# One RNN, one state-space layer, one LSTM and one adapter in a software pipeline: the RNN's lead goes from 56 to 54 steps and the side jobs move to other steps

## The chip, the core and the metric

The kernel runs on one core of one Trainium2 chip. The metric is the device time of one launch in microseconds (us), as the median of several runs. A profile of one execution stands beside it. In it PE is TensorE's matmuls, PEld its weight loads, DVE is VectorE, ACT is ScalarE, POOL is GpSimd and SP the engine that issues most of the DMAs. A line such as L402 is line 402 of the kernel.

## What is computed

The input `x` has 4 sequences of 1024 tokens with 512 features. Four layers follow each other, each added to its input: a tanh RNN, a state-space layer, an LSTM, and an adapter whose weights depend on the condition vector. Cut to what matters, for `h`, `state` and `c` carried from token to token:

```python
# 1. RNN
h = tanh(x_t @ Wx + b + h @ Wh)
# 2. state space; the convolution has the condition vector's rows as its 4 taps
proj = conv(x) @ Wp + bp;  B_t = softplus(proj[:N]);  C_t = tanh(proj[N:])
u = x @ Ws + bs
state = decay * state + dt * B_t * u_t;  y_t = C_t * state;  out = y @ Wo + bo
# 3. LSTM
A = x_t @ Wx + b + h @ Wh
i, f, o, g = sigmoid(A[0:H]), sigmoid(A[H:2H]), sigmoid(A[2H:3H]), tanh(A[3H:4H])
c = f * c + i * g;  h = o * tanh(c)
# 4. adapter: one 512x512 matrix per sequence
out = x @ (base + a(cond) @ b(cond))
```

Everything is float32. The RNN and the LSTM are recurrences of 1024 steps over only 4 rows, so the number of steps and the time of one step set the time of the kernel.

## The kernel before

Time is cut into 32 chunks of `TC` = 32 steps. `do_pass(c)` walks the 32 steps of chunk `c` of the LSTM. The RNN runs `LEAD` = 56 steps ahead of it: in step `t` of pass `c` it does its step number `32c + t + 56`. Before the LSTM has anything to do, one short pass (number -2, 24 steps) and one whole pass (number -1, 32 steps) advance the RNN alone; this prologue also loads weights and computes the adapter's matrices. In pass `c` the layers are staggered: the LSTM works on chunk `c`, the state-space layer on chunk `c + 1`, the RNN's input projections (`project0`) on chunk `c + 3`, the adapter on chunk `c - 1`.

The program's order is written by hand: each engine does its instructions in the order in which the code issues them, and waits where an operand is not there. An LSTM step is cut into two halves of the hidden width, A and B (`Half`, L392). One step issues, in this order (L846 to L898):

- TensorE: the LSTM's 96 bfloat16 matmuls (`lstm_mm`, L374), those of A first as far as A's own h reaches, then those that need B's h; then the step's "pe" jobs; then the RNN's 16 float32 matmuls (`rnn_mm`, L348). In the first steps of the prologue `keep_busy` adds matmuls whose result nobody reads.
- VectorE: for each half a transpose of the accumulator (L402), a sum (L408), the products and the cell (L428, L433), the new h (L441), and h split into bfloat16 parts (L207). Half A's and half B's are interleaved. Behind B's cell come the step's "gap" jobs, then B's h and its splits, then the RNN's transpose and addition (`rnn_pre`, L365), then the "end" jobs. The first instruction of the next step is A's transpose.
- ScalarE: the gates (L415), A's tanh (L438), B's gates, then "gap" jobs, then two copies of the next step's input sums (`lstm_input`, L389), then B's tanh, then the RNN's tanh (L371), then "end" jobs.

A job is a triple of step, place ("pe", "gap" or "end") and function. `do(t, place)` runs those that match, in the order of the list: the adapter's, then the state-space layer's, then the LSTM's input projections of the next chunk, then `load_x`, then `project0`, then the LSTM's input projections of the running chunk. The jobs that the change touches are these:

- `ssm_jobs` (L451): `add` forms the state-space input from x and the RNN's h (L460). `taps` and `skip` are its matmuls. On ScalarE follow L498 and L499, then the exponential L500 and the copy L501, and the output's tanh L502. On VectorE follow four reciprocals of 64x32 (`turn`, L494), two products (L503, L504), and a chain of 14 operations: six of a series (L509), L511, L512, L513, four scans (L516), and the output y (L521). Then come 16 matmuls (`out_mm`) and four additions (`x2_end`, L533).
- `input_jobs` (L797): the LSTM's input projections for eight steps of a chunk: four groups of matmuls (L333), two transposes (`input_turn`, L337), two bias additions of two gates each (`input_bias`, L345). The first eight steps of a chunk are prepared in the pass before it, the others in the same pass.
- `project0` (L309): four groups of 16 matmuls, each with a copy on ScalarE (L321).
- `at_step(i, f)` (L680) puts a job of the prologue at the i-th step counted from the start, which needs `LEAD` to find the pass.

The places of the state-space layer's VectorE work come from two lines:

```python
place = lambda n: ("gap", "end", "end")[n % 3]
jobs += [(19 + (n + 1) // 3, place(n + 1), f) for n, f in enumerate(chain)]
```

Of the kernel before, what the change touches and what calls it, by code (L numbers as in the profile page):

```python
# [10 lines left out]
AF = mybir.ActivationFunctionType  # L11
# [5 lines left out]
KC = D // P  # L17
TC = 32
NCHUNK = T // TC
TOK = TC * B  # L20
TG = 8
LEAD = TC + 24
CT = 32
TAPS = B
NG = 4 * KC
# [1 line left out]
NS = 64  # L27
# [8 lines left out]
SERIES = [1.0 / (2 * n + 1) for n in range(1, 8)]  # L36
# [3 lines left out]
def cond_resid_kernel(ctx: ExitStack, tc: tile.TileContext, a: dict, out: bass.AP):  # L40
# [79 lines left out]
    x1 = state.tile([P, KC, 3 + TC, B], F32, name="x1", tag="x1")  # L120
# [18 lines left out]
    vec = const.tile([P, 4], F32, name="vec", tag="vec")  # L139
# [161 lines left out]
    def bank(name, shape, tag="fill", bufs=2):  # L301
        return psum.tile(shape, F32, name=name, tag=tag, bufs=bufs)

    def tiled(dst, columns, x, first=True, final=True, tiles=4):

        for j in range(tiles):
            nc.tensor.matmul(dst[CT * j : CT * (j + 1)], columns(j), x, start=first, stop=final)  # L307
# [143 lines left out]
    def ssm_jobs(c):  # L451
        x, h, po = xin[c % XBUFS], h0[c % 2], {}
        v, act = nc.vector, nc.scalar

        def sm(name):
            return small.tile([NS, TOK], F32, name=name, tag=name, bufs=1)

        def add(ms, t0, t1):
            t = lambda y: y[:, ms, t0:t1].rearrange("p c t b -> p c (t b)")
            v.tensor_add(t(x1[:, :, 3:, :]), t(x), t(h))  # L460


        jobs = [
            (5, "end", lambda: add(slice(0, 2), 0, TC - 4)),
            (6, "end", lambda: add(slice(2, 4), 0, TC - 4)),
            (7, "end", lambda: add(slice(0, 4), TC - 4, TC)),
        ]
        pb = bank("pb", [P, 2, TOK], tag="pb", bufs=1)


        def taps(k):
            for tap in range(TAPS):
                tiled(
                    pb[:, 0, :], lambda j: wp[:, tap, k, CT * j : CT * (j + 1)], x1[:, k, tap : tap + TC, :],
                    tap == 0 and k == 0, tap == TAPS - 1 and k == KC - 1,
                )

        def skip():
            for k in range(KC):
                tiled(  # L480
                    pb[:, 1, :], lambda j: ws[:, k, CT * j : CT * (j + 1)], x1[:, k, 3:, :],
                    k == 0, k == KC - 1, tiles=NS // CT,
                )

        cg, z, e, u, w, p = (sm(n) for n in ("cg", "z", "e", "u", "w", "p"))
        bt, vv, states, y = z, e, w, p
        v3, y3 = (t.rearrange("p (t b) -> p t b", b=B) for t in (vv, states))
        y_last = y3[:, TC - 1, :]
        jobs += [(8 + 2 * k, "pe", lambda k=k: taps(k)) for k in range(KC)]
        jobs.append((16, "pe", skip))  # L490

        def turn(n):
            cols = slice(n * TOK // 4, (n + 1) * TOK // 4)
            v.reciprocal(u[:, cols], u[:, cols])  # L494


        jobs += [
            (14, "end", lambda: act.activation(z, pb[:NS, 0, :], AF.Identity, bias=vec[:NS, 0:1])),  # L498
            (14, "end", lambda: act.activation(e, pb[:NS, 0, :], AF.Abs, bias=vec[:NS, 0:1])),  # L499
            (15, "end", lambda: act.activation(e, e, AF.Exp, scale=-1.0)),  # L500
            (15, "end", lambda: act.activation(u, e, AF.Copy, bias=2.0)),  # L501
            (18, "end", lambda: act.activation(cg, pb[NS:, 0, :], AF.Tanh, bias=vec[NS:, 0:1])),  # L502
            (18, "end", lambda: v.tensor_mul(u, u, e)),  # L503
            (18, "end", lambda: v.tensor_mul(w, u, u)),  # L504
            (18, "end", lambda: act.activation(p, w, AF.Copy, scale=2.0 * SERIES[-1])),
            (24, "end", lambda: act.copy(s1, y_last)),
        ]

        chain = [lambda q=q: v.scalar_tensor_tensor(p, p, 2.0 * q, w, ALU.add, ALU.mult) for q in SERIES[-2::-1]]  # L509
        chain += [  # L510
            lambda: v.scalar_tensor_tensor(p, p, 2.0, u, ALU.add, ALU.mult),  # L511
            lambda: v.scalar_tensor_tensor(bt, z, 0.0, p, ALU.max, ALU.add),  # L512
            lambda: v.scalar_tensor_tensor(vv, pb[:NS, 1, :], vec[:NS, 1:2], bt, ALU.add, ALU.mult),  # L513
        ]
        for b in range(B):
            chain.append(lambda b=b: v.tensor_tensor_scan(  # L516
                y3[:, :, b], decay, v3[:, :, b], s1[:, b : b + 1], ALU.mult, ALU.add
            ))

        chain += [  # L520
            lambda: v.scalar_tensor_tensor(y, states, dt, cg, ALU.mult, ALU.mult),  # L521
        ]
        place = lambda n: ("gap", "end", "end")[n % 3]
        jobs += [((16, "end"), (16, "end"), (17, "gap"), (17, "end"))[n] + (lambda n=n: turn(n),) for n in range(4)]
        jobs += [(19 + (n + 1) // 3, place(n + 1), f) for n, f in enumerate(chain)]

        def out_mm():
            po[0] = bank("ssm_out", [P, KC, TOK], tag="po", bufs=1)
            for m in range(KC):
                tiled(po[0][:, m, :], lambda j: wo[:, P * j + CT * m : P * j + CT * (m + 1)], y)  # L530

        def x2_end(m):
            v.scalar_tensor_tensor(  # L533
                x2[c % 2][:, m].rearrange("p t b -> p (t b)"), po[0][:, m, :], bo[:, 0, m : m + 1],
                x1[:, m, 3:, :].rearrange("p t b -> p (t b)"), ALU.add, ALU.add,
            )

        jobs += [
            (24, "pe", out_mm),
            *((24 + (m + 1) // 2, ("end", "gap")[m % 2], lambda m=m: x2_end(m)) for m in range(KC)),  # L540
            (26, "end", lambda: act.copy(x1[:, :, 0:3, :], x1[:, :, TC : TC + 3, :])),
        ]
        return jobs

# [64 lines left out]
    def adapt_w2(j):  # L609

        half, hd, rg = j // (KC * RANK // WR), j // (RANK // WR) % KC, j % (RANK // WR) // 2
        ps = bank("pp", [P, P])
        for k in range(KC):
            for t in range(4):
                nc.tensor.matmul(  # L615
                    ps[CT * t : CT * (t + 1), :], hid[:, k, :], w2[j + t // WR][:, t % WR, k],
                    start=(k == 0), stop=(k == KC - 1),
                )
        nc.scalar.copy(xr[:, half, hd, rg], ps)
        for n in range(j + W2_BUFS, min(j + W2_BUFS + 2, NW2)):  # L620
            load_w2(n)
# [55 lines left out]
    def at(c, t, f):  # L677
        early.setdefault((c, t), []).append(f)

    def at_step(i, f):  # L680

        c, t = divmod(i - LEAD, TC)
        at(c, t, f)
# [48 lines left out]
    for j in range(0, NW2, 2):  # L732
        f = lambda j=j: adapt_w2(j)
# [63 lines left out]
    def input_jobs(c, n, steps, turns):  # L797
        ps = {}

        def mm(k):  # L800
            if not ps:

                ps[0] = bank("proj2", [P, D], tag=("ada", "po")[n % 2], bufs=1)
            input_mm(c, n, k, ps[0])

        work = (
            lambda: input_turn(c, n, 0, ps[0]), lambda: input_turn(c, n, 2, ps[0]),
            lambda: input_bias(c, n, 0), lambda: input_bias(c, n, 2),
        )
        return [(t, "pe", lambda k=k: mm(k)) for k, t in enumerate(steps)] + [  # L810
            (t, place, f) for (t, place), f in zip(turns, work)
        ]


    def do_pass(c, first=0, src=None, dst=None, last=None):

        lstm = c >= 0
        jobs = []
# [5 lines left out]
        if -1 <= c < NCHUNK - 1:  # L824
            jobs += ssm_jobs(c + 1)
            jobs += input_jobs(
                c + 1, 0, range(25, 29), ((28, "end"), (29, "gap"), (29, "end"), (30, "gap"))
            )
        if src is not None:
            jobs.append((9, "end", lambda: load_x(c + 4, src)))  # L830
        if c + 3 < NCHUNK:
            for m in range(KC):
                mm, end = project0(c + 3, m)
                t = (18, 20, 22, 30)[m]
                jobs += [(t, "pe", mm), (t, "end", end)]
        if lstm:
            jobs += input_jobs(c, 1, range(4), ((3, "end"), (4, "gap"), (4, "end"), (5, "gap")))
# [8 lines left out]
        for t in range(first, TC):  # L846
            r = divmod(c * TC + t + LEAD, TC)
            rnn = r[0] < NCHUNK
# [54 lines left out]
    for m in range(KC):  # L903
        mm, end = project0(0, m)
        mm()
        end()
    def dst(c):
        return lambda b: out[b, bass.ds(c * TC, TC), :]

    do_pass(-2, first=2 * TC - LEAD)  # L910
    for c in range(-1, NCHUNK):
        if c == 0:
            for m in range(2):
                lstm_input(0, 0, m)
        do_pass(
            c, src=a["xT"][c + 4] if c + 4 < NCHUNK else None, dst=dst(c - 1) if c > 0 else None,
            last=dst(c) if c == NCHUNK - 1 else None,
        )
# [60 lines left out]
```

## Time and profile before

| what | value |
|---|---|
| median of 3 runs | 4686.77 us (4686.28 to 4688.5) |
| profiled execution | 4682.72 us, of which the span is 4680.9 us |
| granted TensorE clock, mean | 0.998 |
| LSTM matmuls (L383) | 98304, busy 2900.4 us |
| RNN matmuls (L352) | 32768, busy 1088.6 us |
| LSTM input projections (L333) | 4096, busy 529.6 us |
| transposes of the accumulator (L402) | 4096, mean 309 ns |
| first transpose of the first LSTM step | 157.8 us from the start |
| first transpose of the last LSTM step | 4667.2 us from the start |

The span is the time from the first to the last instruction that the profile shows; the execution adds 1.8 us around it. The last two rows give the main loop: 1023 steps in 4509.4 us. A matmul of float32 is recorded as two. Busy times are unions over an engine, and ends of matmuls are modelled, so an engine that is shown busy all the time need not be at its limit. A bracket at the end of a line of the timeline gives the idle time of that engine ahead of the instruction, and what ended it.

### The profile page before, as it was taken

To read this page: it belongs to the slowest core of one execution; us is meant where nothing else is said; L and a number is where in the kernel's file an instruction comes from. 1 tells how busy PE (TensorE), PEld (TensorE's weight loads), DVE (VectorE), ACT (ScalarE), POOL (GpSimd) and SP (SyncE) were. 2 spreads that over 40 slices of the span, in tenths; PEclk is the share of its full clock that TensorE was granted. 3 is DMA by queue.
4 is the path that set the end of the run, shared out by engine and by line. 5 is a ranking of instruction groups with operands and counts; after the bars stand their busy time and mean duration, and the time that the engine had idled before them with its cause. 6 is when DMAs were issued, how large, how long until landed. Compare 5 with 4: busy or idle time off the path is not lost.

```text
span 4680.9 us, 326427 instructions
## 1 busy us (share of the span) xinstructions
PE 4546.1 (97%) x146816; PEld 3574.0 (76%) x146816; DVE 3951.6 (84%) x22102; ACT 1876.8 (40%) x9693; POOL 47.9 (1%) x92
## 2 busy tenths in 40 slices
PE   7999999999999999999999999999999999999986
PEld 4777777777777777777777777778777777777754
DVE  4688888888888888888888888888888888888876
ACT  3334444444443444443444444444444444444333
POOL 3000000000000000000000000000000000000000
PEclk9999999999999999999999999999999999999999
DMA  6300000000000000000000000000000000000000
GB/s 151 123 6 8 9 7 9 9 7 9 9 7 9 9 7 9 9 7 9 9 7 9 9 7 9 9 7 9 9 7 9 9 7 9 9 5 7 6 6 8
DMA packets 40235, 67.77 MB, mean 14 GB/s; under 512 B 8864, under 2 KB 26016, under 8 KB 38320
## 3 DMA queue, kind: packets, MB, share of 16 engines
q1 hardware_dynamic: 35792, 46.55, 3.7%
q8 instruction: 1147, 18.79, 1.7%
q14 instruction: 256, 2.10, 0.2%
q0 software_dynamic: 1696, 0.19, 0.0%
q10 hardware_dynamic: 1344, 0.14, 0.0%
HBM read 38.34 MB, written 8.39 MB: 10 GB/s over the span
## 4 chain that ended last, share of the span: by engine, by line
PE 91%; DVE 7%; issue 1%; POOL 0%; DMA 0%; ACT 0%; SPq 0%; DVEq 0%; ACTq 0%; POOLq 0%
PE acc L383 55%; PE acc L352 18%; PE proj L333 9%; PE pb L307 3%; DVE tt L402 3%; DVE gc L408 2%; PE proj L307 2%; PE ada L754 2%; DVE prod L428 1%; PE ssm_out L307 1%; DVE h L207 1%; PE idle L307 0%; PE pp L615 0%; DVE h L441 0%; DVE tt L367 0%
## 5 line engine op out<-in xcount | busy, mean ns | idle before, releaser
L383 PE MATMUL acc<-wh,h 128*12 128x256 bf16 x98304 | 2900.4, 273 | 95.0 <-DVE h L207 92.0
L383 PEld LDWEIGHTS <-h 128*12 128x12 bf16 x98304 | 2312.5, 87 | 545.5 <-DVE h L207 181.9
L402 DVE STREAM_TRANSPOSE tt<-acc 128x192 f32<-128x192 f32 (+1 forms) x4096 | 1233.0, 309 | 285.9 <-PE acc L383 261.5
L415 ACT ACTIVATE gc<-gc 128x24 f32<-128x24 f32 (+1 forms) x4096 | 855.3, 216 | 1386.1 <-DVE gc L408 1379.4
L352 PEld LDWEIGHTS acc<-wh,h 128*4 128x4 f32 x32768 | 808.3, 87 | 507.3 <-issue 204.6
L352 PE MATMUL acc<-wh,h 128*4 128x128 f32 x32768 | 1088.6, 273 | 17.3 <-ACT h L371 12.8
L408 DVE TENSOR_REDUCE gc<-tt 128x24 f32<-128x96 f32 (+1 forms) x4096 | 1037.4, 255 | 70.5
L207 DVE TENSOR_TENSOR h<-h 128x8 f32<-128x8 f32 (+1 forms) x4098 | 671.6, 164 | 69.9
L371 ACT ACTIVATE h<-pre 128x16 f32<-128x16 f32 x1024 | 221.5, 216 | 1126.1 <-DVE pre L368 1126.1
L438 ACT ACTIVATE th<-gc 128x8 f32<-128x8 f32 x2048 | 427.7, 209 | 255.1 <-DVE gc L433 220.1
L333 PE MATMUL proj<-wx,x 128*32 128x512 f32 x4096 | 529.6, 592 | 0.0
L441 DVE SCALAR_TENSOR_TENSOR h<-gc,th 128x8 f32<-128x8 f32 x2048 | 328.5, 160 | 143.6 <-ACT th L438 134.0
L367 DVE STREAM_TRANSPOSE tt<-acc 128x128 f32<-128x128 f32 x1024 | 315.4, 308 | 64.7 <-PE acc L352 64.6
L428 DVE SCALAR_TENSOR_TENSOR prod<-gc 128x16 f32<-128x16 f32 x2048 | 347.7, 170 | 12.6
L390 ACT COPY tt<-xw 128x32 f32<-128x32 f32 x2048 | 327.7, 207 | 0.0
L433 DVE SCALAR_TENSOR_TENSOR gc<-prod 128x8 f32<-128x8 f32 x2048 | 297.4, 145 | 0.0
L368 DVE TENSOR_TENSOR pre<-xw,tt 128x16 f32<-128x16 f32 x1024 | 179.6, 175 | 37.6
L307 PE MATMUL proj<-xin,wx 128*32 128x128 f32 x4096 | 135.1, 274 | 12.0 <-DMA wh<-in_Wh_dram 11.9
L307 PE MATMUL pb<-x,wp 128*32 128x128 f32 x4096 | 136.1, 274 | 1.1 <-issue 0.7
L754 PE MATMUL ada<-layer,x 128*32 128x512 f32 (+1 forms) x1056 | 133.9, 586 | 2.7 <-DVE x L747 2.6
L307 PEld LDWEIGHTS proj<-xin,wx 128*32 128x32 f32 x4096 | 114.7, 111 | 15.9 <-DMA wh<-in_Wh_dram 11.9
L333 PEld LDWEIGHTS proj<-wx,x 128*32 128x32 f32 x4096 | 118.8, 110 | 5.5 <-issue 0.3
(125 smaller groups left out, 1161.6 us busy)
## 6 DMA issues: line engine op xcount, KB each, us to landing
layer<-in_w2T_dram SPq DMA_DIRECT2D x32, 512.0 KB, 4.7
xin<-in_xT_dram SPq DMA_DIRECT2D x128, 64.0 KB, 2.5
out_dram<-x SPq DMA_DIRECT2D x124, 64.0 KB, 2.1
wx<-in_Wx_dram SPq DMA_DIRECT2D x20, 256.0 KB, 5.1
layer<-in_Wh_dram SPq DMA_DIRECT2D x16, 256.0 KB, 4.9
wh<-in_Wh_dram SPq DMA_DIRECT2D x4, 256.0 KB, 8.1
layer<-in_w_dram SPq DMA_DIRECT2D x4, 256.0 KB, 4.6
layer<-in_base_dram SPq DMA_DIRECT2D x4, 256.0 KB, 8.7
```

Source lines behind the costliest of these rows:

```text
L207: nc.vector.tensor_tensor(h[:, :, n], h[:, :, n - 1], upper(h[:, :, n - 1]), ALU.subtract)
L307: nc.tensor.matmul(dst[CT * j : CT * (j + 1)], columns(j), x, start=first, stop=final)
L333: nc.tensor.matmul(ps[CT * j : CT * (j + 1), :], tok, w[:, j], start=(k == 0), stop=(k == KC - 1))
L352: nc.tensor.matmul(acc0[CT * j : CT * j + B, :], h[:, k, (t - 1) % TC, :], wh0[:, k, j * P : (j + 1) * P], start=(k == 0), stop=(k == KC - 1),
L383: nc.tensor.matmul(acc2[mh][CT * j : CT * j + NP * B, :], upper(h[:, k, (t - 1) % TC].rearrange("p s b -> p (s b)")), w[:, :, n0 : n0 + 2 ...
L390: nc.scalar.copy(tt2[m][t % 2][:, :, :, :B], xw2[c % 2][:, :, 2 * m : 2 * m + 2, t, :])
L402: nc.vector.transpose(self.tt[:, g0:g1, :, B:].rearrange("p g c b -> p (g c) b"), acc2[self.m][:, 2 * CT * g0 : 2 * CT * g1],)
L408: nc.vector.tensor_reduce(self.gc[:, to : to + g1 - g0].rearrange("p g c b -> p (g c) b"), self.tt[:, g0:g1, :, : (1 + NP) * B].rearrange( ...
L415: nc.scalar.activation(self.gc[:, g0:g1], self.gc[:, g0:g1], AF.Tanh, scale=0.5)
L428: nc.vector.scalar_tensor_tensor(self.prod, self.gc[:, 0:2], 1.0, self.gc[:, 2:4], ALU.add, ALU.mult)
L438: nc.scalar.activation(self.th, self.c, AF.Tanh, scale=0.5)
L441: nc.vector.scalar_tensor_tensor(self.out[:, :, 0], self.gc[:, 4], 1.0, self.th, ALU.add, ALU.mult)
```

## The change

`LEAD` becomes 54. The prologue's first pass starts two steps later and has 22 steps, and the RNN ends two steps later in the main loop. Since the RNN now finishes a chunk in step 9 of a pass instead of step 7, the three `add` jobs move from the ends of steps 5, 6, 7 to 7, 8, 9, and the matmuls of `taps` and `skip` by two steps. The ScalarE work behind them moves by one or two steps, and L500 and L501 go from the end of a step into the gap of step 17. The reciprocals go from steps 16 and 17 to 17 and 18. L503 goes into the gap of step 19. The chain of 14 operations has four to a step, one in the gap and three at the end, in steps 20 to 23, where it had three to a step in 19 to 23. The output's matmuls move from step 24 to 25, its additions with them, and the input projections of the next chunk's first eight steps by one step, so that their last bias addition lies in the gap of step 31 instead of 30. `project0` goes from steps 18, 20, 22, 30 to 20, 22, 30, 31. No operation is added; of `keep_busy`, two calls fall away with the two steps.

```diff
--- before.py
+++ after.py
@@ -19,7 +19,7 @@
 NCHUNK = T // TC
 TOK = TC * B
 TG = 8
-LEAD = TC + 24
+LEAD = TC + 22
 CT = 32
 TAPS = B
 NG = 4 * KC
@@ -461,9 +461,9 @@
 
 
         jobs = [
-            (5, "end", lambda: add(slice(0, 2), 0, TC - 4)),
-            (6, "end", lambda: add(slice(2, 4), 0, TC - 4)),
-            (7, "end", lambda: add(slice(0, 4), TC - 4, TC)),
+            (7, "end", lambda: add(slice(0, 2), 0, TC - 4)),
+            (8, "end", lambda: add(slice(2, 4), 0, TC - 4)),
+            (9, "end", lambda: add(slice(0, 4), TC - 4, TC)),
         ]
         pb = bank("pb", [P, 2, TOK], tag="pb", bufs=1)
 
@@ -486,8 +486,8 @@
         bt, vv, states, y = z, e, w, p
         v3, y3 = (t.rearrange("p (t b) -> p t b", b=B) for t in (vv, states))
         y_last = y3[:, TC - 1, :]
-        jobs += [(8 + 2 * k, "pe", lambda k=k: taps(k)) for k in range(KC)]
-        jobs.append((16, "pe", skip))
+        jobs += [(10 + 2 * k, "pe", lambda k=k: taps(k)) for k in range(KC)]
+        jobs.append((18, "pe", skip))
 
         def turn(n):
             cols = slice(n * TOK // 4, (n + 1) * TOK // 4)
@@ -495,14 +495,14 @@
 
 
         jobs += [
-            (14, "end", lambda: act.activation(z, pb[:NS, 0, :], AF.Identity, bias=vec[:NS, 0:1])),
-            (14, "end", lambda: act.activation(e, pb[:NS, 0, :], AF.Abs, bias=vec[:NS, 0:1])),
-            (15, "end", lambda: act.activation(e, e, AF.Exp, scale=-1.0)),
-            (15, "end", lambda: act.activation(u, e, AF.Copy, bias=2.0)),
-            (18, "end", lambda: act.activation(cg, pb[NS:, 0, :], AF.Tanh, bias=vec[NS:, 0:1])),
-            (18, "end", lambda: v.tensor_mul(u, u, e)),
-            (18, "end", lambda: v.tensor_mul(w, u, u)),
-            (18, "end", lambda: act.activation(p, w, AF.Copy, scale=2.0 * SERIES[-1])),
+            (16, "end", lambda: act.activation(z, pb[:NS, 0, :], AF.Identity, bias=vec[:NS, 0:1])),
+            (16, "end", lambda: act.activation(e, pb[:NS, 0, :], AF.Abs, bias=vec[:NS, 0:1])),
+            (17, "gap", lambda: act.activation(e, e, AF.Exp, scale=-1.0)),
+            (17, "gap", lambda: act.activation(u, e, AF.Copy, bias=2.0)),
+            (19, "end", lambda: act.activation(cg, pb[NS:, 0, :], AF.Tanh, bias=vec[NS:, 0:1])),
+            (19, "gap", lambda: v.tensor_mul(u, u, e)),
+            (19, "end", lambda: v.tensor_mul(w, u, u)),
+            (19, "end", lambda: act.activation(p, w, AF.Copy, scale=2.0 * SERIES[-1])),
             (24, "end", lambda: act.copy(s1, y_last)),
         ]
 
@@ -520,9 +520,9 @@
         chain += [
             lambda: v.scalar_tensor_tensor(y, states, dt, cg, ALU.mult, ALU.mult),
         ]
-        place = lambda n: ("gap", "end", "end")[n % 3]
-        jobs += [((16, "end"), (16, "end"), (17, "gap"), (17, "end"))[n] + (lambda n=n: turn(n),) for n in range(4)]
-        jobs += [(19 + (n + 1) // 3, place(n + 1), f) for n, f in enumerate(chain)]
+        place = lambda n: ("gap", "end", "end", "end")[n % 4]
+        jobs += [((17, "end"), (17, "end"), (18, "gap"), (18, "end"))[n] + (lambda n=n: turn(n),) for n in range(4)]
+        jobs += [(20 + n // 4, place(n), f) for n, f in enumerate(chain)]
 
         def out_mm():
             po[0] = bank("ssm_out", [P, KC, TOK], tag="po", bufs=1)
@@ -536,9 +536,9 @@
             )
 
         jobs += [
-            (24, "pe", out_mm),
-            *((24 + (m + 1) // 2, ("end", "gap")[m % 2], lambda m=m: x2_end(m)) for m in range(KC)),
-            (26, "end", lambda: act.copy(x1[:, :, 0:3, :], x1[:, :, TC : TC + 3, :])),
+            (25, "pe", out_mm),
+            *((25 + (m + 1) // 2, ("end", "gap")[m % 2], lambda m=m: x2_end(m)) for m in range(KC)),
+            (27, "end", lambda: act.copy(x1[:, :, 0:3, :], x1[:, :, TC : TC + 3, :])),
         ]
         return jobs
 
@@ -824,14 +824,14 @@
         if -1 <= c < NCHUNK - 1:
             jobs += ssm_jobs(c + 1)
             jobs += input_jobs(
-                c + 1, 0, range(25, 29), ((28, "end"), (29, "gap"), (29, "end"), (30, "gap"))
+                c + 1, 0, range(26, 30), ((29, "end"), (30, "gap"), (30, "end"), (31, "gap"))
             )
         if src is not None:
             jobs.append((9, "end", lambda: load_x(c + 4, src)))
         if c + 3 < NCHUNK:
             for m in range(KC):
                 mm, end = project0(c + 3, m)
-                t = (18, 20, 22, 30)[m]
+                t = (20, 22, 30, 31)[m]
                 jobs += [(t, "pe", mm), (t, "end", end)]
         if lstm:
             jobs += input_jobs(c, 1, range(4), ((3, "end"), (4, "gap"), (4, "end"), (5, "gap")))
```

## The prediction, made before the changed kernel ran

> **What bounds the kernel now.** I read the page's busy shares and slices, then the waits, then busy time by single steps of the main loop, then the timeline of those steps. The page alone would mislead:
>
> ```profile
> PE 4546.1 (97%) x146816; PEld 3574.0 (76%) x146816; DVE 3951.6 (84%) x22102; ACT 1876.8 (40%) x9693; POOL 47.9 (1%) x92
> ```
>
> TensorE looks full. Four steps of the 17th chunk say otherwise (columns: window, us, busy of PE, PEld, DVE, ACT, POOL, clock, DMA):
>
> ```profile
> 2525.16:2529.54 4.38, 4.38 (x147) 3.26 (x139) 4.08 (x24) 1.95 (x11) 0.00 (x0) 1.00 0.01 4
> 2529.54:2534.14 4.60, 4.60 (x169) 4.08 (x161) 3.68 (x22) 2.06 (x11) 0.00 (x0) 1.00 0.27 64
> 2551.64:2556.02 4.38, 3.76 (x138) 2.96 (x130) 4.03 (x22) 1.69 (x9) 0.00 (x0) 1.00 0.03 6
> 2556.02:2560.39 4.37, 4.37 (x171) 3.91 (x162) 3.69 (x21) 1.95 (x10) 0.00 (x0) 1.00 0.01 4
> ```
>
> These are steps 23, 24, 29 and 30. Call T the start of a step's first transpose of half A (L402); a step runs from T to the next T. Step 29 has no extra matmul job and TensorE idles 0.62 us in it, yet it lasts 4.38 us like its neighbours. So the recurrence h -> matmuls -> gates -> h takes 4.38 us by itself, and the fills of about 0.5 us only fit into it. Step 24 alone is longer. The timeline of step 29 shows the last link:
>
> ```profile
> 2554.27 0.21 ACT L438 ACTIVATE th<-gc 128x8 f32<-128x8 f32 x1
> 2554.53 0.16 DVE L441 SCALAR_TENSOR_TENSOR h<-gc,th 128x8 f32<-128x8 f32 x1
> 2554.72 0.37 DVE L207 TENSOR_TENSOR h<-h 128x8 f32<-128x8 f32 x2
> 2555.14 0.98 PEld L383 LDWEIGHTS <-h 128*12 128x12 bf16 x40 [0.21 <-DVE h L207]
> 2556.02 0.38 DVE L402 STREAM_TRANSPOSE tt<-acc 128x192 f32<-128x192 f32 x1 [0.17 <-PE acc L383]
> ```
>
> Half B's cell (L433) goes through ACT's tanh (L438) to its h (L441) at T+2.88 and its splits (L207) to T+3.45. TensorE has waited 0.21 us for them, and T comes 0.93 us later. Whatever delays B's h delays T by as much. A "gap" job stands in front of B's h, an "end" job behind rnn_pre and in front of the next T. Their room is read from step 21:
>
> ```profile
> 2518.91 0.28 DVE L509 SCALAR_TENSOR_TENSOR p<-p,w 64x128 f32<-64x128 f32 x1
> 2519.03 0.21 ACT L438 ACTIVATE th<-gc 128x8 f32<-128x8 f32 x1
> 2519.27 0.17 DVE L441 SCALAR_TENSOR_TENSOR h<-gc,th 128x8 f32<-128x8 f32 x1
> ...
> 2520.20 0.28 DVE L511 SCALAR_TENSOR_TENSOR p<-p,u 64x128 f32<-64x128 f32 x1
> 2520.50 0.28 DVE L512 SCALAR_TENSOR_TENSOR z<-z,p 64x128 f32<-64x128 f32 x1
> 2520.78 0.38 DVE L402 STREAM_TRANSPOSE tt<-acc 128x192 f32<-128x192 f32 x1
> ```
>
> T is 2516.39; offsets below are medians of the same steps in 24 chunks. The gap job starts at T+2.52; one of up to 0.44 us is over when tanh delivers, two are not. End jobs start at T+3.80; two fill the time to T exactly. A third has no room, and the second chunk shows what that costs:
>
> ```profile
> 385.88 0.44 DVE L337 STREAM_TRANSPOSE xw<-proj 128x256 f32<-128x256 f32 x1
> ...
> 386.24 0.65 DVE L652 TENSOR_TENSOR layer<-layer,pl 128x512 f32<-128x512 f32 x1
> ...
> 386.82 0.36 DVE L402 STREAM_TRANSPOSE tt<-acc 128x192 f32<-128x192 f32 x1
> ```
>
> That step began at 382.08 and took 4.73 us: T came 0.07 us before the recorded end of the last end job. The following one took 4.35, so only 0.03 came back.
>
> **What the Trainium skill says.** "Perfetto Trace Analysis", section Optimizing Scalar/DVE Operations: the write-acknowledging half of an instruction overlaps with the next; the 0.07 above agrees. Its section Identifying the Most-Contended Engine warns that matmul busy time does not tell the distance to the limit; step 29 agrees. "ScalarE: Activation LUTs", What ACT_TABLE_LOAD costs: consecutive ACTIVATEs overlap by about 93 ns; here L390's two start 0.11 apart at 0.21 each, so 0.10. "TensorEngine Tiling (Array Packing)", Key Properties: changing the tiling mode drains TensorE. It bears on step 24 (below), and the trace fits it.
>
> **The change, step by step.** All sums are per chunk, against 4.38 us a step.
>
> - Step 8: an end job L460 (0.38) now precedes L337 (0.44): 3.80, 4.10 to 4.54, less 0.08: 4.46, so +0.08.
> - Step 9: the last L460 waits for that step's RNN tanh (in step 7 of before it started at T+4.16, with nothing behind it). Now L345 (0.42) is queued behind it: 4.30 to 4.72, T at 4.64, +0.26.
> - Step 17: L500 (0.29) and, dependent on it, L501 (0.31) move into ACT's gap, ahead of both L390 and B's tanh. From T+2.27: 2.56, then 2.60 to 2.91, L390 from 2.81 and 2.92, tanh at 3.03 instead of 2.63: +0.40. Without the overlap +0.52. Nothing covers it; step 15 hid them behind the RNN's tanh.
> - Step 18: gap holds L494 (0.34) and L345 (0.42): 2.51, 2.77 to 3.19, B's h at 3.12 instead of 2.88: +0.24.
> - Step 19: gap holds L503 (0.28) and L345: B's h at 3.06: +0.18. The remaining L504 fits at the end.
> - Steps 20 and 21: three dependent end jobs of 0.28, 0.31 apart, end at 4.70: T at 4.62, +0.24 each.
> - Step 22: three scans, 0.20 apart, end at 4.47: +0.01. Step 23: nothing.
> - Step 31: L345 for gates 2 and 3 of the next chunk's first steps is now in this step's gap (2.51 to 2.93), and L390 at the end of the same step reads that tile. Before, it lay in step 30. ACT, in order, holds B's tanh behind it: L390 from 2.96 and 3.07, tanh at 3.18 instead of 2.63: +0.55.
> - Output: the one long step moves from 24 to 25, 0. I don't credit its 0.22 us, because y was not late:
>
> ```profile
> 2529.26 0.34 DVE L521 SCALAR_TENSOR_TENSOR p<-w,sp,cg 64x128 f32<-64x128 f32 x1
> 2530.51 0.81 PEld L307 LDWEIGHTS ssm_out<-p,wo 64*32 64x32 f32 x32 [0.22 <-DVE tt L402]
> ```
>
> y ended at 2529.60, 0.91 us before. ssm_out's weights have 64 rows where all neighbours have 128, and the idle 0.2 comes again when the rows go back; a drain explains both. Bounds: 0 to -0.22.
> - Moved projections, taps, adds out of steps 5 and 6: each is still one fill of 0.5 us to a step, two steps (8 and 24) now have none, and step 29 shows that an empty one gains nothing. load_x on SP still follows the add that frees its buffer.
>
> Sum: 0.08+0.26+0.40+0.24+0.18+0.24+0.24+0.01+0.55 = 2.20 us. Of the 31 passes that have it, the first hides step 9 in its adapter step of 5.22 us and gains at step 23: 1.7. The last has no RNN from step 10 on, so steps 20 and 21 fit: 1.7. 29 x 2.20 + 3.4 = 67.2 us.
>
> Prologue: 54 steps instead of 56, at the commonest 2.0 us (one tanh of the RNN to the next): -4.0. One pp matmul job slips into the first LSTM step (5.2 instead of 4.4 us, as its odd neighbours; less 0.6 in the prologue): +0.2. The out_mm no longer waits 1.28 us for y: -1.4. Together -5.2; -11 to +1, since TensorE's half-clock stretch near 106 to 118 us may move. At the other end two LSTM steps get an RNN: they last 4.38 either way, 0.
>
> Total +62. The profiled execution took 4682.72 us (span 4680.9), which gives 4744.7; it lies 4.05 below the median of the runs, so the median should be 4748.8, say **4749**.
>
> **Rivals.**
> - Faster. The 0.22 us of ssm_out is a late y, and a whole step of lead ends it: -0.22 x 31 = -7.0, with -5.2 of the prologue 4674.6. DVE's idle 0.3 to 0.9 us a step would have to take in the rest; it decides as long as the jobs cost under 0.22 + 5.2/31 = 0.39 us a chunk. Against it: y's 0.91 us, and idle time that lies in waits for tanh and TensorE, where a later job doesn't fit.
> - Slower by a third of it. B's chain has slack in filled steps, and only the end jobs count (8, 9, 20, 21): 0.82 x 31 - 5 = +20, 4707. Against it: steps 29 and 31, where B's chain alone gives 4.38.
> - Slower by more: delays that compound, or step 17 and 31 without overlap: 2.7 x 31 + 1 = +85, 4772 and over.
> - The jobs fall evenly and the sum is within 0.2% (9.4 us, about what can be told from no change).
>
> **How the numbers follow.** My case 0.78, with its own range 4725 (stall of ssm_out gone, 0.3 less a chunk) to 4772; a third of it 0.08; more 0.05; faster 0.06; same 0.03. The range 4705 to 4775 takes in the first two. Slower 0.91, same 0.03, faster 0.06.
>
> **What would show it.** Steps 17 and 31 at about 4.8 and 4.9, with ACT's tanh waiting for nothing but L390; 18 to 21 and 9 at 4.55 to 4.65; step 24 at 4.38 and 25 at 4.60; everything else unchanged; T of the first LSTM step (157.8) some 5 us earlier. If 25 is 4.38, the drain is wrong; if 18, 19 and 31 are 4.38, B's chain is not the limit.

## The result, and the profile after

| | before | after |
|---|---|---|
| median | 4687.64 us (4686.28 to 4689.56, 4 runs) | 4751.47 us (4747.31 to 4751.98, 4 runs) |
| ratio | 1 | 1.0137, 95% interval 1.0124 to 1.0149 |
| span of the profiled execution | 4680.9 us | 4745.5 us |

The change makes the kernel 1.4% slower. The page hides it as well as it hid the limit before; TensorE's share of the span is the same 97%:

```profile
PE 4582.1 (97%) x146800; PEld 3557.4 (75%) x146800; DVE 3939.9 (83%) x22102; ACT 1878.0 (40%) x9693; POOL 47.3 (1%) x92
```

Two rows of the view of waits tell more (who waits for whom: us in total, times, longest). Before:

```profile
PEld L383 <- DVE h L207: 181.9, 309, 1.8
```

After:

```profile
PEld L383 <- DVE h L207: 295.4, 672, 1.8
ACT tt L390 <- DVE xw L345: 21.2, 31, 0.9
```

TensorE's wait for the LSTM's split h has grown. The last row is new: once in each of 31 passes ScalarE's copy of the next step's input waits for a bias addition.

Where the time is comes out of the busy times of single steps, here 8, 17, 20, 24, 25 and 31 of the 17th chunk (window, us, busy of PE, PEld, DVE, ACT, POOL, clock, DMA):

```profile
2491.50:2495.98 4.48, 3.85 (x140) 3.02 (x132) 4.30 (x24) 1.70 (x9) 0.00 (x0) 1.00 0.02 4
2531.26:2536.04 4.78, 4.52 (x147) 3.25 (x138) 3.88 (x23) 2.36 (x12) 0.00 (x0) 1.00 0.02 3
2545.11:2549.76 4.65, 4.65 (x180) 4.12 (x172) 4.31 (x24) 2.53 (x12) 0.00 (x0) 1.00 0.01 4
2563.13:2567.52 4.39, 3.76 (x138) 2.94 (x129) 3.43 (x20) 2.07 (x11) 0.00 (x0) 1.00 0.27 67
2567.52:2572.13 4.61, 4.61 (x170) 4.09 (x162) 3.68 (x22) 1.70 (x9) 0.00 (x0) 1.00 0.02 4
2594.02:2599.04 5.02, 4.54 (x170) 3.86 (x161) 3.77 (x21) 1.96 (x11) 0.00 (x0) 1.00 0.03 7
```

In step 20 PE is shown busy for all 4.65 us, as it was for all 4.38 us of the filled steps of before, although the step got no matmul job beyond its fill. So a busy PE does not tell whether TensorE sets the time of a step. Steps 8, 17 and 31 show TensorE idle, and 24 and 25 have exchanged their roles. The medians over 24 chunks (4 to 27), each step taken from half A's first transpose to the next one:

| step | before, us | after, us | difference | foretold |
|---|---|---|---|---|
| 8 | 4.382 | 4.475 | +0.09 | +0.08 |
| 9 | 4.375 | 4.598 | +0.22 | +0.26 |
| 17 | 4.376 | 4.783 | +0.41 | +0.40 |
| 18 | 4.388 | 4.546 | +0.16 | +0.24 |
| 19 | 4.380 | 4.529 | +0.15 | +0.18 |
| 20 | 4.385 | 4.649 | +0.26 | +0.24 |
| 21 | 4.382 | 4.616 | +0.23 | +0.24 |
| 22 | 4.387 | 4.372 | -0.02 | +0.01 |
| 24 | 4.605 | 4.388 | -0.22 | -0.22 |
| 25 | 4.371 | 4.604 | +0.23 | +0.22 |
| 31 | 4.379 | 5.025 | +0.65 | +0.55 |

No other step moves by more than 0.03 us. All 32 differences add up to 2.20 us a chunk. Over the whole execution: start to the first LSTM step -10.1 us, first chunk +9.9, chunks 1 to 31 +64.4, the rest +0.3; together the 64.6 us between the spans.

The timeline of step 17 shows how a gap job on ScalarE reaches TensorE (start, duration; in brackets idle time and what ended it):

```profile
2533.53 0.29 ACT L500 ACTIVATE e<-e 64x128 f32<-64x128 f32 x1
...
2533.85 0.31 ACT L501 ACTIVATE u<-e 64x128 f32<-64x128 f32 x1
...
2534.07 0.32 ACT L390 COPY tt<-xw 128x32 f32<-128x32 f32 x2
2534.29 0.20 ACT L438 ACTIVATE th<-gc 128x8 f32<-128x8 f32 x1
2534.53 0.17 DVE L441 SCALAR_TENSOR_TENSOR h<-gc,th 128x8 f32<-128x8 f32 x1 [0.68 <-ACT th L438]
...
2535.15 0.98 PEld L383 LDWEIGHTS <-h 128*12 128x12 bf16 x40 [0.55 <-DVE h L207]
```

The tanh's operand, the cell, was ready at 2533.85; the tanh started 0.44 us later, behind the two jobs and the two copies that are issued ahead of it. VectorE then waits 0.68 us for it, and the loading of TensorE's weights 0.55. The step is 0.41 us longer. Step 31 has the same form with a different beginning:

```profile
2596.55 0.42 DVE L345 TENSOR_TENSOR xw<-xw,b 128x256 f32<-128x256 f32 x1
...
2597.06 0.34 ACT L390 COPY tt<-xw 128x32 f32<-128x32 f32 x2 [0.66 <-DVE xw L345]
2597.30 0.21 ACT L438 ACTIVATE th<-gc 128x8 f32<-128x8 f32 x1
2597.54 0.17 DVE L441 SCALAR_TENSOR_TENSOR h<-gc,th 128x8 f32<-128x8 f32 x1 [0.57 <-ACT th L438]
```

ScalarE idles 0.66 us for an addition that VectorE has been given for this very gap, and the tanh that VectorE needs next stands behind the waiting copy.

### The profile page after: what moved, and what is told of

Its sections match the earlier page's. It is cut to its first block, busy times and chain, and to the rows that moved or that the text cites. A ratio compares the mean times of both kernels' runs of the same rounds, so it can differ in the third digit from the quotient of the medians.

```text
span 4745.5 us, 326418 instructions
## 1 busy us (share of the span) xinstructions
PE 4582.1 (97%) x146800; PEld 3557.4 (75%) x146800; DVE 3939.9 (83%) x22102; ACT 1878.0 (40%) x9693; POOL 47.3 (1%) x92
## 4 chain that ended last, share of the span: by engine, by line
PE 86%; DVE 11%; ACT 1%; issue 1%; POOL 0%; DMA 0%; SPq 0%; DVEq 0%; ACTq 0%; POOLq 0%
PE acc L383 53%; PE acc L352 17%; PE proj L333 9%; DVE tt L402 4%; DVE gc L408 3%; PE pb L307 3%; PE proj L307 2%; PE ada L754 2%; DVE h L207 1%; DVE prod L428 1%; PE ssm_out L307 1%; DVE h L441 1%; ACT tt L390 0%; PE idle L307 0%; DVE gc L433 0%
## 5 line engine op out<-in xcount | busy, mean ns | idle before, releaser
L307 PE MATMUL proj<-xin,wx 128*32 128x128 f32 x4096 | 135.8, 275 | 11.5 <-DMA wx<-in_Wx_dram 11.5
L307 PE MATMUL pb<-x,wp 128*32 128x128 f32 x4096 | 134.6, 273 | 1.3 <-DVE x L460 1.3
L307 PEld LDWEIGHTS proj<-xin,wx 128*32 128x32 f32 x4096 | 115.3, 111 | 15.4 <-issue 13.5
```

## The experiments

The theory: the LSTM's recurrence through half B sets the step, so a job costs what it overruns its place by. Its rival: idle time of VectorE and ScalarE takes the jobs in, and the loss has another source (the shorter lead itself, the moved matmuls). All ratios are to the kernel before as it was measured beside each run; its median was 4681.76 us for the first four experiments and 4681.46 us for the others.

**ScalarE's gap alone.** In the kernel before:

```diff
-(15, "end", lambda: act.activation(e, e, AF.Exp, scale=-1.0)),
-(15, "end", lambda: act.activation(u, e, AF.Copy, bias=2.0)),
+(15, "gap", lambda: act.activation(e, e, AF.Exp, scale=-1.0)),
+(15, "gap", lambda: act.activation(u, e, AF.Copy, bias=2.0)),
```

> The kernel before with one part of the change alone: L500 and L501 go from the end of step 15 into its gap, ahead of the copies L390 and half B's tanh. If half B's chain sets the step (the prediction's theory), step 15 goes from 4.385 us to 4.78 to 4.80, all others stay, and the total rises by 0.40 x 31 = 12.4 us, from 4687 to about 4700. If ScalarE's idle 60% takes such work in (the rival), step 15 stays at 4.39 and the total at 4687.

Measured: 4695.22 us, +13.5; ratio 1.0029 (1.0017 to 1.0041). The median of step 15 is 4.794 us and no other step moved. In the 17th chunk:

```profile
2496.28:2501.07 4.79, 4.53 (x146) 3.22 (x138) 3.78 (x21) 2.36 (x13) 0.00 (x0) 1.00 0.02 3
```

ScalarE is busy 2.36 of 4.79 us, and still the two instructions cost 0.41 us. The rival fails here.

**The late bias alone.** In the kernel before:

```diff
-c + 1, 0, range(25, 29), ((28, "end"), (29, "gap"), (29, "end"), (30, "gap"))
+c + 1, 0, range(25, 29), ((28, "end"), (29, "gap"), (29, "end"), (31, "gap"))
```

> The kernel before with another part alone: the last bias addition of the next chunk's first eight steps goes from the gap of step 30 to that of step 31, where the copy L390 of the same step reads its tile. Theory: step 31 goes from 4.38 to 5.0 us (the changed kernel shows 5.03), though the step has no extra matmuls here; total +0.65 x 31 = +20 us, to about 4707. Rival, that the 5.03 us in the changed kernel come from the projection which it put into step 31: step 31 stays at 4.38 and the total at 4687. The first LSTM pass's step 31 tells of the projection: 7.87 us in the changed kernel, 4.65 before; here about 5.3 if the projection causes the rest.

Measured: 4700.93 us, +19.2; ratio 1.0043 (1.0028 to 1.0058). Step 31 has a median of 5.004 us:

```profile
2569.88:2574.89 5.01, 3.85 (x140) 2.97 (x131) 3.75 (x22) 1.71 (x10) 0.00 (x0) 1.00 0.02 3
```

With 3.85 us of PE and no fill the step is within 0.02 us as long as in the changed kernel. Step 31 of the first LSTM pass is a case of its own: it took 4.64 us before, 7.87 in the changed kernel and 5.01 here. So the 7.87 has a second cause, which a run further down takes up.

**Three operations to a step.** In the changed kernel:

```diff
-place = lambda n: ("gap", "end", "end", "end")[n % 4]
+place = lambda n: ("gap", "end", "end")[n % 3]
...
-jobs += [(20 + n // 4, place(n), f) for n, f in enumerate(chain)]
+jobs += [(20 + n // 3, place(n), f) for n, f in enumerate(chain)]
```

> The changed kernel with the chain at three operations to a step (one in the gap, two at the end, steps 20 to 24) instead of four. Theory: steps 20 and 21 go from 4.65 and 4.62 back to 4.38; the total falls by (0.265 + 0.235) x 30 = 15 us, from 4751 to about 4736. y now ends directly ahead of the step with the output's matmuls; if a late y makes that step long, step 25 grows above 4.60; if the change of rows in TensorE does, it stays at 4.60. If the end jobs are not what costs (rival: only the gap jobs do), 20 and 21 stay and the total too.

Measured: 4733.84 us; ratio 1.0114 (1.0098 to 1.0129), where the changed kernel has 1.0137. In the traces chunks 1 to 31 take 4403.8 us instead of 4418.9, 15.1 less. Steps 20, 21 and 25:

```profile
2540.91:2545.30 4.39, 4.39 (x171) 3.92 (x163) 4.09 (x24) 2.38 (x12) 0.00 (x0) 1.00 0.02 4
2545.30:2549.67 4.37, 4.37 (x145) 3.25 (x137) 4.07 (x24) 1.83 (x10) 0.00 (x0) 1.00 0.02 6
2562.83:2567.43 4.60, 4.60 (x169) 4.08 (x161) 3.67 (x21) 1.70 (x9) 0.00 (x0) 1.00 0.01 4
```

So the third end job was the cost in these two steps. Step 25 is 4.60 us with y a whole step ahead (changed kernel) and with y just ahead (here), so lateness of y is not what makes it long.

**128 rows for the output.** In the kernel before, `ypad` is a tile of 128 rows whose lower 64 hold y; the upper rows of it and of `wo` are zero:

```diff
-wo = const.tile([NS, D], F32, name="wo", tag="wo")
+wo = const.tile([P, D], F32, name="wo", tag="wo")
+ypad = const.tile([P, TOK], F32, name="ypad", tag="ypad")
...
-tiled(po[0][:, m, :], lambda j: wo[:, P * j + CT * m : P * j + CT * (m + 1)], y)
+tiled(po[0][:, m, :], lambda j: wo[:, P * j + CT * m : P * j + CT * (m + 1)], ypad)
```

> The kernel before with the output's 16 matmuls over 128 rows instead of 64: the weights wo and y have 64 more rows of zeros, all else is as it was. If a drain at the change from 128 to 64 rows and back makes step 24 long, it goes from 4.605 to 4.38 and the total falls by 0.22 x 32 = 7 us, to about 4680. If y's wait or the output's own work does, step 24 stays at 4.60 and the total at 4687.

Measured: 4676.03 us; ratio 0.9989 (0.9980 to 0.9997). Step 24 and its first weights:

```profile
2530.27:2534.66 4.39, 4.39 (x171) 3.90 (x163) 3.69 (x23) 2.06 (x11) 0.00 (x0) 1.00 0.27 67
```

```profile
2531.03 0.88 PEld L310 LDWEIGHTS ssm_out<-ypad,wo 128*32 128x32 f32 x32
```

(L310 is L307 of the other kernels.) The weights now start 0.76 us after the step's beginning without a wait, where they started after 0.97 us. When the row count does not change, the step is 0.22 us shorter, though the matmuls multiply twice as many rows. In chunks 1 to 31 the traces of two runs show 5.3 and 6.3 us less, where 7 were expected. The Trainium skill, "TensorEngine Tiling (Array Packing)", Key Properties, states that a change of tiling mode drains TensorE. The run fits that, with a price of 0.22 us for there and back in this step. What it shows is that the change of rows costs; that this is a change of mode, and the drain itself, stand in no record.

**Gap and end jobs pulled apart.** In the changed kernel:

```diff
-range(4, 8), ((8, "gap"), (8, "end"), (9, "gap"), (9, "end"))
+range(4, 8), ((8, "gap"), (9, "gap"), (10, "gap"), (10, "end"))
...
-range(9, 17, 2), ((15, "end"), (16, "gap"), (18, "gap"), (19, "gap"))
+range(9, 17, 2), ((15, "end"), (16, "gap"), (16, "end"), (17, "gap"))
```

> The changed kernel with the LSTM's transposes and biases for steps 16 to 31 moved out of steps 8, 9, 18, 19 (to 8 gap, 9 gap, 10 gap, 10 end; 15 end, 16 gap, 16 end, 17 gap). Theory: no step has two gap jobs or three end jobs but 20 to 22; 8, 9, 18 and 19 go from 4.475, 4.60, 4.55 and 4.53 back to 4.38; step 17 keeps its 4.78, though it now has a gap job of VectorE too, because tanh comes 0.40 us late anyway; total 0.62 x 31 = 19 us under the changed kernel. Rival: the reciprocals and products themselves cost there; then 18 and 19 stay.

Measured: 4733.1 us; ratio 1.0105 (1.0092 to 1.0119). Steps 8, 9, 18 and 19 have medians of 4.387, 4.379, 4.379 and 4.387 us, step 17 has 4.795. Chunks 1 to 31 take 16.5 us less than in the changed kernel, where 19 were expected: the medians give the foretold 0.62 us a chunk, but single longer steps take some back, the largest 1.0 us in the first step of chunk 1, where TensorE's clock is in part at half speed. Steps 17 and 18:

```profile
2528.46:2533.26 4.80, 4.53 (x147) 3.23 (x139) 4.23 (x24) 2.37 (x13) 0.00 (x0) 1.00 0.01 3
2533.26:2537.64 4.38, 4.38 (x156) 3.97 (x147) 3.92 (x23) 1.69 (x9) 0.00 (x0) 1.00 0.02 4
```

The same operations, at most two steps from where they were, cost nothing in any of the four steps, so the reciprocals and products are not costly in themselves.

**The projection out of step 31.** In the changed kernel:

```diff
-t = (20, 22, 30, 31)[m]
+t = (20, 22, 24, 30)[m]
```

> The changed kernel with the projections in steps 20, 22, 24, 30 instead of 20, 22, 30, 31. Theory: in the main loop nothing moves, step 31 stays at 5.02 us without extra matmuls and step 24 at 4.38 with them. In the first LSTM pass, step 31 falls from 7.87 to about 5.3 us, because the adapter's matmuls no longer wait 2.4 us for the projection's copy L321, and the total falls by 2.6 us. Rival: step 31's 5.02 us need the projection; then it falls to 4.38.

Measured: 4743.65 us in one run, too few for a difference of 2.6 us; the span is 4741.9 us. In the main loop step 31 stays at 5.008 and step 24 is 4.404 us with the fill. In the first pass step 31 falls from 7.87 to 5.00 us. What it had waited for is in the trace of the changed kernel:

```profile
309.76 0.29 PEld L659 LDWEIGHTS pl<-xt,xt 8*128 8x128 f32 x2 [2.40 <-ACT xw L321]
```

The adapter's matmuls and the projections take turns in the same two banks (`bank`, L301, with its default of two buffers), and the projection that the change put into this step frees its bank only when ScalarE copies it at the step's end.

**Everything within its room.** The changed kernel with the chain at three a step, the gap and end jobs apart, the projection in step 24 and the 128 rows, all as above; with L500 and L501 at the end of step 17, the reciprocals in 18 and 19, L503 at the end of 19, and the last bias addition cut so that what step 31's copy reads is done at the end of step 30:

```diff
-(17, "gap", lambda: act.activation(e, e, AF.Exp, scale=-1.0)),
+(17, "end", lambda: act.activation(e, e, AF.Exp, scale=-1.0)),
...
-((17, "end"), (17, "end"), (18, "gap"), (18, "end"))[n]
+((18, "gap"), (18, "end"), (18, "end"), (19, "gap"))[n]
...
-lambda: input_bias(c, n, 0), lambda: input_bias(c, n, 2),
+lambda: input_bias(c, n, 0),
+*([lambda: input_bias(c, n, 2)] if n else
+  [lambda: input_bias(c, n, 2, 0, 1), lambda: input_bias(c, n, 2, 1, TG)]),
...
-((29, "end"), (30, "gap"), (30, "end"), (31, "gap"))
+((29, "end"), (30, "gap"), (30, "end"), (30, "end"), (31, "gap"))
```

> The changed kernel (RNN's lead 54, output in step 25) with every job back within its room: the chain at three a step; L500 and L501 at the end of step 17, the reciprocals after them in 18 and 19; the LSTM's transposes and biases out of the crowded steps 8, 9, 18, 19; the last bias cut in two, so that step 31's gap holds only what the copy of that step does not read; the last projection in the empty step 24 instead of 31; the output over 128 rows. Theory: every step of chunks 4 to 27 at 4.38 us. Against the kernel before with 128 rows alone, the loop after the first chunk is the same; the shorter lead leaves only what the start gains: T of the first LSTM step about 7 us earlier (151.7 and 147.7 against 155.4 to 157.8 in the profiles so far), less what the first chunk loses again, 4 to 6 us. So 0 to 4 us under the kernel with 128 rows and 6 to 11 us under the kernel before. If the lead itself lengthens the loop (rival), steps stay above 4.38 somewhere.

Beside it ran the kernel before with 128 rows once more:

> The kernel before with the output over 128 rows, once more, on the same chip as the repaired kernel, so that the two can be compared: steps at 4.38 us throughout, 7 us under the kernel before if the loop alone counts (the first time 5.7 us).

Measured: 4679.6 us, ratio 0.9993 (0.9985 to 1.0001), against 4676.45 us, ratio 0.9988 (0.9982 to 0.9995). Every step of the repaired kernel has a median between 4.37 and 4.41 us. So the 2.2 us a chunk belong to the places of the jobs and not to the lead. But the repaired kernel is 3 us above the kernel with 128 rows where 0 to 4 us below was expected. Two things are visible. The gain at the start is missing in its profile: the first LSTM step began at 156.1 us, not near 150. And chunks 1 to 31 take 4351.5 us against 4348.3 and 4349.2 in the two runs with 128 rows, about 0.1 us a chunk more, spread over many steps. Whether the lead or one of the moved jobs has this small price was not tested. The version that beats both kernels is the kernel before with 128 rows, by 0.1% in two runs.

**The start, from all ten profiles.** Times of the first LSTM step and of the second chunk's first, in us:

| kernel | lead | first LSTM step | second chunk |
|---|---|---|---|
| before | 56 | 157.8 | 312.7 |
| exponential in gap | 56 | 156.7 | 314.2 |
| late bias | 56 | 155.4 | 312.3 |
| 128 rows, two runs | 56 | 157.2, 156.4 | 316.6, 312.0 |
| changed | 54 | 147.7 | 312.6 |
| three to a step | 54 | 151.7 | 315.3 |
| projection in 24 | 54 | 149.0 | 310.4 |
| gaps apart | 54 | 149.7 | 317.6 |
| all repaired | 54 | 156.1 | 315.8 |

With the shorter lead the LSTM starts 4 to 10 us earlier in four of five profiles, and the first chunk is longer by about as much. The second chunk begins at 312.0 to 316.6 us with the long lead and at 310.4 to 317.6 us with the short one; the scatter among kernels of one lead is larger than any gain. Each figure comes from one execution, and in two of them (three to a step, gaps apart) 3.4 and 6.8 us at half of TensorE's clock lie where the first chunk ends.

## Why the prediction was right, and where its sizes were off

The direction and the size came from one reading, that step 29 of before lasts 4.38 us with 0.62 us of idle TensorE. The isolated moves of the exponential and of the bias show that half B's chain passes a delay on at once, and the third end job and the two gap jobs show the same for VectorE's order. Foretold were 4749 us and 2.20 us a chunk; measured were 4751.47 us and 2.20. That the sums agree so closely is in part luck: the misses of single steps, from -0.08 us in step 18 to +0.10 in step 31, cancel. In the list, T is the start of a step, as in the prediction.

- Step 17 (+0.40): right, with the overlap of about 0.10 us between ScalarE's instructions that the trace of before had shown; the case without it, 0.52, did not occur.
- Steps 20 to 22 and 8: right within 0.03 us.
- Step 9 (+0.26): 0.22, since step 8, itself overrun, hands it 0.04 us back: in step 9 all VectorE times lie 0.04 us earlier against its start.
- Steps 18 and 19 (+0.24, +0.18): 0.16 and 0.15. B's h came at T+3.06 and T+3.04 instead of the usual 2.88. In 18 the mis-sized term is L345's start-to-end time behind a reciprocal, 0.35 us instead of 0.42. A rest of about 0.02 us was room that the empty step had not shown.
- Step 31 (+0.55): 0.65. The copy was taken to start 0.03 us after the addition's recorded end, as the tanh does after the cell (2.60 to 2.63). It started 0.09 us after it (2.95 to 3.04), which is the larger part of the miss. The same 0.09 stands in the run with the bias alone (2.93 to 3.02), so it belongs to this wait and not to the projection.
- Output (0): right, and the reason too: the long step moved from 24 to 25 with its 0.22 us, and went with the change of rows.
- Prologue and first chunk: here the sizes failed. Foretold were -5.2 us for the start and +1.7 for the first chunk, together -3.5; measured were -10.1 and +9.9, together -0.1. Of the first chunk, 2.4 us is the bank that the adapter's matmuls waited for in step 31; the prediction had no term for it, though the moved projection and the adapter share their banks. Steps 0 to 2 give another 3.7 us: the loading of TensorE's weights stands there for 4.7 us without a releaser that the profile shows ("issue"), up to 1.6 us at a time, against 1.6 us in all before. The adapter's weights arrive in the same time, but no run tests whether they are the cause. About 2 us more are spread over other steps. Why the start and the first chunk trade time so evenly was not settled.
- The start and the clock: the prediction allowed -11 to +1 us for the prologue, because a stretch at half clock might move, and such stretches did move. Between 90 us and the first LSTM step the clock record has 10.2 us at half speed before (6.8 from 110.1 us on, 3.4 from 137.4 on) and none in the changed kernel. Half of that, 5.1 us, is the most that it can have cost TensorE, an estimate, and about the size of the miss. With 54 steps of lead the start comes in the order of this time: none and 147.7 us in the changed kernel, 3.4 with the projection in step 24 and with the gaps apart (149.0 and 149.7), 6.8 with three to a step (151.7), 10.2 in the repaired one (156.1). With 56 steps there is no such order (3.4 to 10.2 us at half speed, starts at 155.4 to 157.8). So part of the -10.1 us of this one execution may be chance; whether the stretches delay the start or only go with it was not tested.

The miss of the start and the first chunk, +3.4 us together, is what the total of the profiled execution was off by, less about 1 us in the loop. Against the range it was small, because some 30 chunks of 2.2 us stand against one start.

## What to carry to other kernels

When a loop lasts as long in a step without extra work as in one with it (4.38 us here), its recurrence is likely the limit, and an engine's idle time is only usable in the places where the recurrence leaves it. The test is to move one job alone, as the first two experiments do. Then list for each place how long it is, and what stands behind it on that engine. A moved job has to be followed in two directions: what is queued behind it, and who reads its result how soon (the copy in step 31), which banks included. A contraction over fewer rows than its neighbours' can cost more than the same one padded with zeros (0.22 us more here).

## What the runs showed that was not expected

Padding 64 rows to 128 made the output's matmuls cheaper in place: step 24 went from 4.605 to 4.384 us. A ScalarE instruction that waits for a VectorE addition of 128x256 started 0.09 us after its recorded end, against 0.03 us after the cell's 128x8. An addition of 128x256 is recorded with 0.35 us behind a reciprocal of 64x32 and with 0.42 us behind the cell. And two steps of lead, which looked like 4 us, bought nothing measurable by the time the second chunk began, and the loop that keeps every job in its room was still 0.1 us a chunk longer than the one with the longer lead.
